# Two attention blocks on one core: a list scheduler that runs in rounds and orders by latest start

## The chip, the cores and the metric

The kernel runs on one core of one Trainium2 chip. A core has a matrix engine (TensorE, PE in the profile, with its weight loads as PEld), a vector engine (DVE), a scalar engine (ACT), a general engine (POOL) and a queue engine (SP) that issues most of the transfers. The metric is the time of one execution on the device in microseconds, as the median of several runs; lower is better.

## The reference

Two conditioned attention blocks follow each other, both over x with 8 batches, 512 positions and 512 features. Each has its own weights. Cut to what matters:

```python
# block 0: linear attention, 8 heads of 64
xn = ln(x)
q = softmax(heads(xn @ Wq + bq), axis=features)
k = softmax(heads(xn @ Wk + bk + mask), axis=positions)
v = heads((xn @ Wv + bv) * mask)
y = q @ (k^T v)
x = x + silu(ln(y) * (1 + scale) + shift) @ W_out + b_out     # scale, shift from silu(emb) @ W_emb
# block 1: full attention, 16 heads of 32
xn = ln(x)
att = softmax(q k^T + mask, axis=keys)
y = att @ v
out = x + silu(ln(y) * (1 + scale) + shift) @ out_w + out_b
```

## The kernel before

**Tiles.** A batch is four chunks of 128 positions by 512 features. Float32 products of projections are made of three passes in the fast float32r format (`project`, line 743): high parts by high, high by low, low by high, 12 matmuls of 512 columns for one output tile.

**Block 0** goes batch by batch: keys and their softmax, values, the 64x64 products of keys and values, queries, outputs.

**Block 1** goes by head groups: G = 4b + g is batch b and its group g of four heads, 32 groups in all. For each group

- `l1_qk` (930) projects keys and queries and writes their high and low parts (hl) to DRAM (dWk, dWq); `l1_stack` (945) loads them back as stacks kst and qst, three buffers each;
- `l1_max` (956) makes scores in the S banks, 16 matmuls, and DVE takes each one's row maximum (nm, a TENSOR_REDUCE). The maxima of a group, split in two parts (mi), are transposed, copied to z, and a small transfer writes them as extra rows into the query stack (qst<-z);
- `l1_att` (982) makes the transposed scores in the ST banks, 16 matmuls, with the maxima subtracted by those extra rows, and ACT takes the exponential into A buffers;
- `l1_av` (1003) multiplies four exponentials with the values, as four matmuls of 32 output rows each that lie side by side in the array (tile a; the trace has two matmul instructions for each, so eight in a group). The exponentials of the later chunks are added onto those of the first (A<-A,A, on POOL or DVE, whichever the planner picks);
- `l1_den` (1032) multiplies those sums with a selector (eg) for the denominators (tile d), again four narrow matmuls.

Beside it run the projections of the next batch and the tail of the one before (transposes, tanh, output product, residual), in the mm banks.

**What sets the order.** Nothing is issued while the program above runs. Every call goes to `Order` (172), which records an operation with its engine, the tiles that it touches and a planned duration from `_takes` (381). A `together` block (186) makes one operation of several matmuls, with a duration given by hand. At the end `place` (262) plays the whole program through: an operation is offered when its dependences are placed and its buffers free; a tag's buffers go out strictly in program order; among the operations that an engine could start, it takes the one with the lowest key, and the key is the place in the program (`o.seq`). A transfer is planned with 560 ns of issue, then a shared rate of 330 bytes per ns and 1700 ns to land. `issue` (361) then writes out every engine's instructions in the order of the planned start; the chip follows this order on each engine and queue. A later user of a tile depends in the plan on that tile's first user (`touch`, 237), transfers included. All instructions have line 370 in the profile, that of the one call that issues them:

```python
engine = getattr(nc, o.takes[o.engine][0])
for method, args, kw in o.calls:
    args = [a.real() if isinstance(a, View) else a for a in args]
    kw = {k: v.real() if isinstance(v, View) else v for k, v in kw.items()}
    getattr(engine, method)(*args, **kw)
```

Buffers: 11 of A, 4 of xc (x and y chunks), 3 of y, 1 of z, 6 of the large stk (raw weights, stacks). Banks: 2 of mm, 2 of S, 2 of ST, 1 of a, 1 of d.

The program starts with block 0's first batch: x and the raw weights (rawL0Wk and so on) are loaded on SP, the small rows of layer norm weights, biases and masks (A<-in_L_cond_ln_b, A<-in_mask_BxSx_fk) too (`load_cols`, 455), and `prep_cols` (468) transposes these and copies them to cols.

Of the kernel before, what the change touches and what calls it, by code (L numbers as in the profile page):

```python
# [4 lines left out]

# [66 lines left out]
class Tile:  # L72
    def __init__(self, pool, tag, shape, dtype, name):
        self.pool, self.tag, self.shape, self.dtype, self.name = pool, tag, tuple(shape), dtype, name
        self.slot, self.ap, self.seen, self.left, self.end = None, None, [], 0, 0.0
        self.view = View(self, (), _index(self.shape), dtype)

    def root(self):
# [13 lines left out]
        return ap  # L92


class View:
# [3 lines left out]
    def _then(self, what, args, kw, at, dtype=None):  # L99
        return View(self.tile, self.chain + ((what, args, kw),), at, dtype or self.dtype)  # L100

    def __getitem__(self, i):
        return self._then("__getitem__", (i,), {}, self.at[i])

    def rearrange(self, pattern, **sizes):
        return self._then("rearrange", (pattern,), sizes, _rearranged(self.at, pattern, sizes))

    def bitcast(self, dtype):
        return self._then("bitcast", (dtype,), {}, self.at, dtype)

    def unsqueeze(self, d):
        return self._then("unsqueeze", (d,), {}, np.expand_dims(self.at, d))

    def broadcast_to(self, shape):
        return self._then("broadcast_to", (shape,), {}, np.broadcast_to(self.at, shape))

    def box(self):
        row = int(np.prod(self.tile.shape[1:]))
        p, c = self.at // row, self.at % row
        return int(p.min()), int(p.max()), int(c.min()), int(c.max())  # L120

    def real(self):
        ap = self.tile.root()
        for what, args, kw in self.chain:
            ap = getattr(ap, what)(*args, **kw)
        return ap


class Pool:
    def __init__(self, order, pool, dram=False, psum=False, each=1, mixed=()):  # L130
        self.order, self.pool, self.dram, self.psum = order, pool, dram, psum
        self.mixed, self.each, self.bufs, self.tiles, self.home = mixed, each, {}, {}, {}

    def tile(self, shape, dtype, name, tag=None, bufs=None):
        tag = name if self.dram else tag or name
# [28 lines left out]
    )  # L164


LINK = {"PE": 55.0, "ACT": 36.0, "DVE": 36.0, "POOL": 90.0, "SP": 60.0}
WEIGHTS = 110.0
DMA_ISSUE, DMA_LAND, DMA_RATE = 560.0, 1700.0, 330.0


class Order:
# [37 lines left out]
    def add(self, name, calls, takes, late, nbytes=0):  # L210
        if not isinstance(takes, dict):
            takes = {name: takes}
        o = Op()
        o.seq, o.calls, o.late, o.bytes = len(self.ops), calls, late, nbytes
        o.takes = {ENGINES[k]: (k, v) for k, v in takes.items()}
        o.deps, o.users, o.tiles, o.fresh = set(), [], [], []
        o.start = o.end = o.engine = None
        o.key = o.seq if self.key is None else self.key
        for t in self.hold:
            self.touch(o, t, None, True)  # L220
        self.hold = []
        for method, args, kw in calls:
            outs, ins = [args[0]], list(args[1:])
            for k, v in kw.items():
                (outs if k == "accum_out" else ins).append(v)
            for v in ins:
                if isinstance(v, View):
                    self.touch(o, v.tile, v.box(), False)
            for v in outs:
                if isinstance(v, View):  # L230
                    box = v.box()
                    if method == "matmul":
                        box = (*box[:2], 0, 511)
                    self.touch(o, v.tile, box, True)
        self.ops.append(o)

    def touch(self, o, t, box, write):
        if t not in o.tiles:
            o.tiles.append(t)
            if t.left:  # L240
                o.deps.add(t.first)
            else:
                o.fresh.append(t)
                t.first = o
            t.left += 1
        if box is None:
# [12 lines left out]
        kept.append((o, box, write))  # L259
        t.seen = kept  # L260

    def place(self):

        now = {e: 0.0 for e in ENGINES.values()}
        ready = {e: [] for e in now}
        later = {e: [] for e in now}
        slots = {}
        dma = 0.0
        for p in self.pools:
            for tag in p.tiles:  # L270
                n = len(p.tiles[tag]) if p.dram else p.bufs[tag]
                slots[p, tag] = [[(0.0, i) for i in range(n)], 0, {}]
        for o in self.ops:
            o.waits = len(o.deps)
            for d in o.deps:
                d.users.append(o)

        def offer(o):

            asked = {}  # L280
            for t in o.fresh:
                room = slots[t.pool, t.tag]
                n = asked.get((t.pool, t.tag), 0)
                if t.place != room[1] + n or len(room[0]) <= n:
                    room[2][room[1] if t.place == room[1] + n else t.place] = o
                    return
                asked[t.pool, t.tag] = n + 1
            at = 0.0
            for t in o.fresh:
                room = slots[t.pool, t.tag]  # L290
                free, t.slot = heapq.heappop(room[0])
                room[1] += 1
# [7 lines left out]
            for e in o.takes:  # L300
                heapq.heappush(later[e], (at, o.seq, o))
            for t in o.fresh:
                room = slots[t.pool, t.tag]
                nxt = room[2].pop(room[1], None)
                if nxt is not None:
                    offer(nxt)

        for o in self.ops:
            if not o.waits:
                offer(o)  # L310
        done = 0
        while done < len(self.ops):
            best = None
            for e in now:
                while later[e] and later[e][0][0] <= now[e]:
                    _, _, o = heapq.heappop(later[e])
# [13 lines left out]
                if best is None or at < best[0]:  # L330
                    best = (at, e, o)
            assert best, "nothing can be placed"
            at, e, o = best
            o.engine, o.start = e, at
            takes = o.takes[e][1]
            if e == "PE" and at > now[e] + 1.0:
                o.start += WEIGHTS
                at = o.start
            now[e] = at + takes
            if o.late is None:  # L340
                dma = max(dma, now[e]) + o.bytes / DMA_RATE
# [4 lines left out]
            for t in o.tiles:  # L346
                t.left -= 1
                t.end = max(t.end, o.end)
                if not t.left:
                    room = slots[t.pool, t.tag]  # L350
                    heapq.heappush(room[0], (t.end + 60.0, t.slot))
                    nxt = room[2].pop(room[1], None)
                    if nxt is not None:
                        offer(nxt)
            for u in o.users:
                u.waits -= 1
                if not u.waits:
# [23 lines left out]
def _takes(engine, method, args, kw):  # L381
# [30 lines left out]
def kernel(ctx: ExitStack, tc: tile.TileContext, x, cond, mask0, mask1, w0, w1, out):  # L412
# [947 lines left out]
```

## Time and profile before

| | before |
|---|---|
| median of 3 runs | 1522.73 us (1520.66 to 1522.84) |
| the profiled execution | 1527.23 us |
| its span, first to last instruction | 1525.2 us |
| mean granted TensorE clock | 0.970 |
| PE busy | 1430.8 us (94%) |
| DVE busy | 1076.0 us (71%) |
| DMA moved | 156.65 MB, mean 103 GB/s |

A row of groups reads: line, engine, operation, output and inputs by name, shapes, count, then busy time, the mean of one in ns, and the idle time ahead of it with what ended it. A row of waits reads: who waited, for whom, microseconds in total, times, the longest. A row of the timeline reads: start, length, instruction, and in brackets the idle time ahead of it.

### The profile page before, as it was taken

Reading aid. Unit: us, or ns where it says so; the run is one execution under the profiler, and the core shown is the slowest. Engines: PE = TensorE matmul, PEld = TensorE weight load, DVE = VectorE, ACT = ScalarE, POOL = GpSimd, SP = SyncE. Lnnn points to the kernel's source line nnn. Section 1 sums busy time; section 2 is a strip of 40 time slices with the busy share of each in tenths; the row PEclk is TensorE's granted clock in tenths of the full one; section 3 lists DMA queues with packets and bytes.
Section 4 is the critical chain, followed back from the end, with each engine's and each line's share of the span. In section 5 each row is a group of like instructions: output and inputs, shape, how many; then the busy total and the mean of one; then the engine's idle time right before and its main releaser. Section 6 shows DMA issues by size and latency. Waiting matters only on the chain.

```text
span 1525.2 us, 20716 instructions
## 1 busy us (share of the span) xinstructions
PE 1430.8 (94%) x7385; PEld 963.0 (63%) x7385; DVE 1076.0 (71%) x1844; ACT 691.3 (45%) x1302; POOL 623.6 (41%) x671
## 2 busy tenths in 40 slices
PE   5899999999999998999899999899999999999997
PEld 2688878888887675545556556455556556656545
DVE  6366655666667677888767678767777867867886
ACT  3223423333335233545555554554545555655562
POOL 3212214124122233455445545445344654554661
PEclk9899999999999998999899999999899999999998
DMA  8014102022121274442263352444435435425311
GB/s 290 13 55 139 52 32 84 1 83 77 63 84 63 86 221 110 143 120 67 86 172 87 108 156 73 134 125 109 122 107 132 126 85 157 127 74 161 86 55 46
DMA packets 76475, 156.65 MB, mean 103 GB/s; under 512 B 8670, under 2 KB 8782, under 8 KB 76372
## 3 DMA queue, kind: packets, MB, share of 16 engines
q1 hardware_dynamic: 73920, 150.99, 33.8%
q10 hardware_dynamic: 2164, 4.24, 0.8%
q8 instruction: 58, 0.95, 0.3%
q14 instruction: 45, 0.37, 0.1%
q0 software_dynamic: 288, 0.10, 0.0%
HBM read 102.67 MB, written 50.40 MB: 100 GB/s over the span
## 4 chain that ended last, share of the span: by engine, by line
PE 77%; DVE 12%; DMA 6%; ACT 2%; issue 1%; POOL 1%; SPq 0%; ACTq 0%; DVEq 0%; POOLq 0%
PE mm L370 46%; PE S L370 11%; PE ST L370 9%; PE a L370 9%; DVE nm L370 4%; DMA qst<-z 3%; DVE A L370 2%; PE d L370 2%; DVE y L370 1%; DVE mi L370 1%; DVE v L370 1%; DMA xc<-in_x 1%; DVE xc L370 1%; ACT A L370 1%; DMA weL<-in_L_cond_W_emb 1%
## 5 line engine op out<-in xcount | busy, mean ns | idle before, releaser
L370 POOL TENSOR_TENSOR A<-A,A 128x512 f32<-128x512 f32 x213 | 303.1, 1439 | 319.4 <-PE a L370 177.6
L370 DVE TENSOR_REDUCE nm<-S 128x1 f32<-128x512 f32 x510 | 339.2, 684 | 101.4 <-PE S L370 99.2
L370 ACT ACTIVATE A<-ST 128x512 f32<-128x512 f32 x448 | 258.9, 603 | 179.0 <-PE ST L370 163.7
L370 PE MATMUL S<-kst,qst 98*128 98x512 f32 x510 | 217.2, 440 | 23.2 <-DVE nm L370 20.3
L370 PE MATMUL ST<-qst,kst 106*128 106x512 f32 x512 | 213.5, 434 | 14.9 <-DMA qst<-z 12.7
L370 PEld LDWEIGHTS S<-kst,qst 98*128 98x128 f32 x510 | 97.5, 194 | 115.1 <-DVE nm L370 76.2
L370 PEld LDWEIGHTS ST<-qst,kst 106*128 106x128 f32 x512 | 96.5, 194 | 86.9 <-ACT A L370 30.5
L370 PE MATMUL a<-A,v 128*32 128x512 f32 x896 | 144.6, 643 | 0.9 <-DVE v L370 0.9
L370 POOL TENSOR_TENSOR y<-y,bo 128x512 f32<-128x512 f32 x60 | 79.6, 1333 | 131.9 <-DMA y<-in_x 90.7
L370 DVE TENSOR_TENSOR A<-A,A 128x512 f32<-128x512 f32 x107 | 104.9, 982 | 39.1 <-PE a L370 31.6
L370 PE MATMUL mm<-xT,Wkh 128*128 128x512 f32 x384 | 118.9, 412 | 6.7 <-DVE cols L370 6.0
L370 PE MATMUL mm<-Wvh,xT 128*128 128x512 f32 x384 | 118.1, 407 | 2.0 <-ACT v L370 1.6
L370 DVE TENSOR_TENSOR y<-y,mm 128x512 f32<-128x512 f32 x60 | 41.1, 685 | 84.4 <-PE mm L370 61.8
L370 PEld LDWEIGHTS mm<-xT,Wkh 128*128 128x128 f32 x384 | 71.9, 194 | 25.1 <-DVE cols L370 6.5
L370 PEld LDWEIGHTS mm<-Wvh,xT 128*128 128x128 f32 x384 | 70.7, 189 | 20.0 <-ACT v L370 2.8
L370 DVE SCALAR_TENSOR_TENSOR v<-bWv,cols,v 128x512 f32<-128x512 f32 x64 | 57.7, 901 | 34.1 <-ACT v L370 33.7
L370 PE MATMUL mm<-Woh,h 128*128 128x512 f32 x224 | 76.0, 437 | 3.8 <-ACT h L370 3.8
L370 ACT ACTIVATE v<-mm,cols 128x512 f32<-128x512 f32 x64 | 44.2, 691 | 71.0 <-PE mm L370 71.0
L370 PE MATMUL mm<-xT,Wqh 128*128 128x512 f32 x256 | 74.5, 398 | 0.0
L370 ACT ACTIVATE hl<-mm,bcol 128x512 fp32r<-128x512 f32 x64 | 43.9, 686 | 62.8 <-PE mm L370 50.8
L370 POOL MEMSET bWk<- 64x4 f32 (+1 forms) x24 | 5.8, 243 | 159.3 <-PE ST L370 158.6
L370 DVE SCALAR_TENSOR_TENSOR hl<-mm,bcol,hl 128x512 fp32r<-128x512 f32 x64 | 47.7, 745 | 27.8 <-ACT hl L370 27.3
(228 smaller groups left out, 2784.2 us busy)
## 6 DMA issues: line engine op xcount, KB each, us to landing
kst<-dWk SPq DMA_DIRECT2D x96, 256.0 KB
qst<-dWq SPq DMA_DIRECT2D x96, 256.0 KB
dWk<-hl SPq DMA_DIRECT2D x32, 512.0 KB
dWq<-hl SPq DMA_DIRECT2D x32, 512.0 KB
xc<-in_x SPq DMA_DIRECT2D x32, 256.0 KB
y<-in_x SPq DMA_DIRECT2D x32, 256.0 KB
x<-y SPq DMA_DIRECT2D x32, 256.0 KB
xc<-x SPq DMA_DIRECT2D x32, 256.0 KB
```

The lines of the kernel that those rows point to most:

```text
L370: getattr(engine, method)(*args, **kw)
```

## The change

`place` now runs up to 12 rounds. Each round plays the program through (`pack`, the old `place` with its keys), then `slack` goes backward over the finished plan and gives every operation as its new key the latest time at which it could start without making the end later, with gaps kept for each engine; the next round orders by these keys. The round with the earliest planned end is kept. The planner also counts, on PE, the cost of going into a group of narrow matmuls and out of it. Some durations change. `l1_den` is no longer an operation of its own: its four matmuls are put ahead of the four of the next head group's first product, in one operation. `Room` replaces the list that hands out buffers; it can hand them out in another order for tags that a pool names as `loose`, and no pool names one. The views' index arrays are cached on the host.

```diff
+ENTER, LEAVE = 95.0, 150.0
+ROUNDS = 12
 LINK = {"PE": 55.0, "ACT": 36.0, "DVE": 36.0, "POOL": 90.0, "SP": 60.0}
...
+class Room:
+    def __init__(self, n, loose):
+        self.free, self.loose, self.head, self.gone, self.queue = [(0.0, i, None) for i in range(n)], loose, 0, set(), {}
+    def lets(self, place, taken):
+        free = len(self.free) - taken
+        if place == self.head + taken:
+            return free > 0
+        return self.loose and free > 1
...
-    def place(self):
+    def place(self, rounds=ROUNDS):
+        best = None
+        for _ in range(rounds):
+            end = self.pack()
+            if best is None or end < best[0]:
+                best = end, [(o.start, o.end, o.engine, [t.slot for t in o.fresh]) for o in self.ops]
+            self.slack(end)
...
+    def slack(self, end):
+        free = {e: [end] for e in ENGINES.values()}
+        for o in sorted(self.ops, key=lambda o: (o.end, o.seq), reverse=True):
+            takes, spent = o.takes[o.engine][1], o.end - o.start
+            t = end - spent
+            for u in o.users:
+                lag = spent + LINK[u.engine]
+                if o.late is not None and o.engine == u.engine:
+                    lag = takes
+                t = min(t, u.key - lag)
+            for x in o.tiles:
+                if x.next is not None:
+                    t = min(t, x.next.first.key - spent - 60.0)
+            o.key = self.latest(free[o.engine], t, takes)
...
-            if e == "PE" and at > now[e] + 1.0:
-                o.start += WEIGHTS
-                at = o.start
+            if e == "PE":
+                many = len(o.calls) > 1
+                if at > now[e] + 1.0:
+                    o.start += WEIGHTS
+                elif many != narrow:
+                    o.start += ENTER if many else LEAVE
+                narrow, at = many, o.start
...
-        return max(62.0, n * (0.447 if args[1].dtype == F32R else 1.668))
+        return max(62.0, n * (0.455 if args[1].dtype == F32R else 1.668))
...
         if n < 64:
-            return 200.0
+            return 400.0 if args[0].tile.tag == "mi" else 200.0
         t = 150.0 + 1.045 * n
         if method == "scalar_tensor_tensor":
             t += 65.0
         if method == "tensor_tensor" and not any(isinstance(a, View) and a.tile.pool.psum for a in ins):
             t += 135.0
+            if args[0].tile.tag == "A":
+                t += 60.0
+        if method == "scalar_tensor_tensor" and not any(isinstance(a, View) and a.tile.pool.psum for a in ins):
+            t += 100.0
         return t
     if engine == "POOL":
         if n < 64:
-            return 1020.0 if ALU.pow in args else 195.0
-        return {"tensor_tensor": 2.66, "tensor_scalar": 1.6}.get(method, 1.03) * n
+            return 900.0 if ALU.pow in args else 350.0
+        return {"tensor_tensor": 2.75, "tensor_scalar": 1.6}.get(method, 1.03) * n
...
     def l1_av(G, m):
         b, g = divmod(G, 4)
-        if m == 0 and G > 0:
-            l1_den(G - 1)
...
-        with order.together(985.0):
+        with order.together(845.0 if m or not G else 1690.0):
+            if m == 0 and G > 0:
+                l1_den(G - 1)
             for j in range(4):
...
     def l1_den(G):
-        with order.together(900.0):
-            for j in range(4):
-                nc.tensor.matmul(
-                    den[32 * j : 32 * j + 32, :], eg[:, g, :], acc[j], start=(g == 0), stop=(g == 3)
-                )
+        for j in range(4):
+            nc.tensor.matmul(
+                den[32 * j : 32 * j + 32, :], eg[:, g, :], acc[j], start=(g == 0), stop=(g == 3)
+            )
...
     l1_av(NG - 1, NC - 1)
-    l1_den(NG - 1)
+    with order.together(845.0):
+        l1_den(NG - 1)
```

More of the change, by code (lines that the diff above doesn't have):

```diff
@@ L2 @@
 import re
+from bisect import bisect_left
 from contextlib import ExitStack, contextmanager
@@ L74, in __init__ @@
         self.pool, self.tag, self.shape, self.dtype, self.name = pool, tag, tuple(shape), dtype, name
-        self.slot, self.ap, self.seen, self.left, self.end = None, None, [], 0, 0.0
+        self.slot, self.ap, self.seen, self.left, self.end, self.next = None, None, [], 0, 0.0, None
         self.view = View(self, (), _index(self.shape), dtype)
@@ L92, in root @@
         return ap
+_SEEN = {}
 class View:
@@ L97, in __init__, with _then @@
         self.tile, self.chain, self.at, self.dtype, self.shape = tile, chain, at, dtype, at.shape
[L99 to L100 removed]
+    def _then(self, what, args, kw, find, dtype=None):
+        chain = self.chain + ((what, args, tuple(kw.items())),)
+        key = self.tile.shape, chain
+        if key not in _SEEN:
+            _SEEN[key] = find()
+        return View(self.tile, chain, _SEEN[key], dtype or self.dtype)
     def __getitem__(self, i):
[L103 removed]
+        return self._then("__getitem__", (i,), {}, lambda: self.at[i])
     def rearrange(self, pattern, **sizes):
[L106 removed]
+        return self._then("rearrange", (pattern,), sizes, lambda: _rearranged(self.at, pattern, sizes))
     def bitcast(self, dtype):
[L109 removed]
+        return self._then("bitcast", (dtype,), {}, lambda: self.at, dtype)
     def unsqueeze(self, d):
[L112 removed]
+        return self._then("unsqueeze", (d,), {}, lambda: np.expand_dims(self.at, d))
     def broadcast_to(self, shape):
[L115 removed]
+        return self._then("broadcast_to", (tuple(shape),), {}, lambda: np.broadcast_to(self.at, shape))
     def box(self):
[L118 to L120 removed]
+        key = self.tile.shape, self.chain, "box"
+        if key not in _SEEN:
+            row = int(np.prod(self.tile.shape[1:]))
+            p, c = self.at // row, self.at % row
+            _SEEN[key] = int(p.min()), int(p.max()), int(c.min()), int(c.max())
+        return _SEEN[key]
     def real(self):
@@ L124, in real, with __init__ @@
         for what, args, kw in self.chain:
-            ap = getattr(ap, what)(*args, **kw)
+            ap = getattr(ap, what)(*args, **dict(kw))
         return ap
 class Pool:
-    def __init__(self, order, pool, dram=False, psum=False, each=1, mixed=()):
+    def __init__(self, order, pool, dram=False, psum=False, each=1, mixed=(), loose=()):
         self.order, self.pool, self.dram, self.psum = order, pool, dram, psum
-        self.mixed, self.each, self.bufs, self.tiles, self.home = mixed, each, {}, {}, {}
+        self.loose, self.mixed, self.each, self.bufs, self.tiles, self.home = loose, mixed, each, {}, {}, {}
     def tile(self, shape, dtype, name, tag=None, bufs=None):
@@ L169, with take, next @@
 DMA_ISSUE, DMA_LAND, DMA_RATE = 560.0, 1700.0, 330.0
+class Room:
[6 more added lines that the diff above has]
+        return self.loose and free > 1
+    def take(self, place):
+        self.gone.add(place)
+        while self.head in self.gone:
+            self.gone.discard(self.head)
+            self.head += 1
+        return heapq.heappop(self.free)
+    def next(self):
+        if self.free and self.head in self.queue:
+            return self.queue.pop(self.head)
+        if self.loose and len(self.free) > 1 and self.queue:
+            return self.queue.pop(min(self.queue))
 class Order:
@@ L234, in add @@
                     self.touch(o, v.tile, box, True)
+        for d in o.deps:
+            d.users.append(o)
         self.ops.append(o)
@@ L243, in touch @@
                 o.fresh.append(t)
-                t.first = o
+                t.first, t.count = o, 0
             t.left += 1
+            t.count += 1
         if box is None:
@@ L260, in touch, with latest, pack @@
         t.seen = kept
-    def place(self):
+    def place(self, rounds=ROUNDS):
[5 more added lines that the diff above has]
+            self.slack(end)
+        for o, (o.start, o.end, o.engine, slots) in zip(self.ops, best[1]):
+            for t, t.slot in zip(o.fresh, slots):
+                pass
+        return best[0]
+    def slack(self, end):
[12 more added lines that the diff above has]
+            o.key = self.latest(free[o.engine], t, takes)
+    @staticmethod
+    def latest(gaps, t, takes):
+        i = min(bisect_left(gaps, t + takes), len(gaps) - 1)
+        i += i % 2
+        while True:
+            hi = min(gaps[i], t + takes)
+            lo = gaps[i - 1] if i else -1e12
+            if hi - takes >= lo:
+                break
+            i -= 2
+        if hi == gaps[i]:
+            gaps[i] = hi - takes
+            if gaps[i] == lo:
+                del gaps[i - 1 : i + 1]
+        else:
+            gaps[i : i + 1] = [hi - takes, hi, gaps[i]]
+        return hi - takes
+    def pack(self):
         now = {e: 0.0 for e in ENGINES.values()}
@@ L267, in place @@
         slots = {}
-        dma = 0.0
+        dma, narrow = 0.0, False
         for p in self.pools:
@@ L271, in place @@
                 n = len(p.tiles[tag]) if p.dram else p.bufs[tag]
-                slots[p, tag] = [[(0.0, i) for i in range(n)], 0, {}]
+                slots[p, tag] = Room(n, tag in p.loose)
         for o in self.ops:
-            o.waits = len(o.deps)
-            for d in o.deps:
-                d.users.append(o)
+            o.waits, o.start = len(o.deps), None
+            for t in o.fresh:
+                t.left, t.end, t.next = t.count, 0.0, None
         def offer(o):
@@ L282, in offer @@
                 room = slots[t.pool, t.tag]
-                n = asked.get((t.pool, t.tag), 0)
-                if t.place != room[1] + n or len(room[0]) <= n:
-                    room[2][room[1] if t.place == room[1] + n else t.place] = o
+                n = asked.get(room, 0)
+                if not room.lets(t.place, n):
+                    room.queue[t.place] = o
                     return
-                asked[t.pool, t.tag] = n + 1
+                asked[room] = n + 1
             at = 0.0
@@ L290, in offer @@
                 room = slots[t.pool, t.tag]
-                free, t.slot = heapq.heappop(room[0])
-                room[1] += 1
+                free, t.slot, before = room.take(t.place)
+                if before is not None:
+                    before.next = t
                 at = max(at, free)
@@ L302, in offer, with again @@
             for t in o.fresh:
[L303 to L306, printed above, removed]
+                again(slots[t.pool, t.tag])
+        def again(room):
+            nxt = room.next()
+            if nxt is not None:
+                offer(nxt)
         for o in self.ops:
@@ L312, in place @@
         while done < len(self.ops):
-            best = None
+            pick = None
             for e in now:
@@ L329, in place @@
                     continue
[L330 to L333, printed above, removed]
+                if pick is None or at < pick[0]:
+                    pick = (at, e, o)
+            assert pick, "nothing can be placed"
+            at, e, o = pick
             o.engine, o.start = e, at
             takes = o.takes[e][1]
-            if e == "PE" and at > now[e] + 1.0:
-                o.start += WEIGHTS
-                at = o.start
+            if e == "PE":
[5 more added lines that the diff above has]
+                narrow, at = many, o.start
             now[e] = at + takes
@@ L350, in place @@
                     room = slots[t.pool, t.tag]
[L351 to L354, printed above, removed]
+                    heapq.heappush(room.free, (t.end + 60.0, t.slot, t))
+                    again(room)
             for u in o.users:
```

## The prediction

> **What bounds the kernel now.** I read the page first: busy shares, the slices, then the chain that ended last.
>
> ```profile
> PE 1430.8 (94%) x7385; PEld 963.0 (63%) x7385; DVE 1076.0 (71%) x1844; ACT 691.3 (45%) x1302; POOL 623.6 (41%) x671
> ...
> PE   5899999999999998999899999899999999999997
> ...
> PEclk9899999999999998999899999999899999999998
> ...
> PE 77%; DVE 12%; DMA 6%; ACT 2%; issue 1%; POOL 1%; SPq 0%; ACTq 0%; DVEq 0%; POOLq 0%
> ```
>
> TensorE is the bound: 94% busy and 77% of the chain; DVE, the next, is at 71%. A plan can only remove TensorE's holes and what the holes cost. PEclk dips at the same slices at which PE does. Next, the busy time by stage:
>
> ```profile
> 0.00:48.00 48.00, 26.13 (x70) 13.50 (x71) 28.20 (x53) 14.06 (x23) 17.75 (x50) 0.86 0.70 239
> 48.00:560.00 512.00, 507.90 (x3015) 406.32 (x3014) 321.08 (x658) 178.95 (x308) 129.24 (x208) 1.00 0.22 74
> 560.00:1440.00 880.00, 825.58 (x3972) 502.28 (x3971) 661.98 (x1032) 455.70 (x883) 437.42 (x380) 0.96 0.42 116
> 1440.00:1526.00 86.00, 71.17 (x334) 40.86 (x332) 64.76 (x104) 42.59 (x89) 39.16 (x34) 0.92 0.19 58
> ```
>
> The columns are the stretch, its length, then busy time of PE, weight load, DVE, ACT, POOL, then granted clock. The start has 21.9 us of PE idle (48 - 26.13), layer 0 has 4.1, the attention stage 54.4, the end 14.8: 95 us in all. Layer 0 is full; there is nothing to win there. Then PE's waits:
>
> ```profile
> PE S L370 <- DVE nm L370: 20.3, 37, 1.8
> PE ST L370 <- DMA qst<-z: 12.7, 13, 5.0
> ...
> PE S L370 <- DVE mi L370: 7.9, 8, 1.7
> ```
>
> In the attention stage PE waits for DVE's row maxima (nm), for what DVE makes of them (mi), and for the small transfer that carries them back into the query stack (z). Then the clock, in two stretches right behind holes of 1.3 us each (849.90 and 1226.10 in the timeline), and the start:
>
> ```profile
> 850.00:856.80 6.80, 6.68 (x18) 3.02 (x19) 5.26 (x9) 2.01 (x4) 3.29 (x3) 0.50 0.55 128
> 1225.40:1232.20 6.80, 6.10 (x18) 3.11 (x18) 2.54 (x6) 2.05 (x4) 5.18 (x7) 0.51 0.09 14
> ...
> 29.37 0.32 SPq L370 DMA_DIRECT2D A<-in_mask_BxSx_fk  x1
> ...
> 34.65 0.31 PE L370 MATMUL mm<-ident,A 48*128 48x48 f32 x1 [5.06 <-DMA A<-in_mask_BxSx_fk]
> ...
> 41.69 0.80 PE L370 MATMUL mm<-xT,Wkh 128*128 128x512 f32 x1 [6.00 <-DVE cols L370]
> ```
>
> A short hole is followed by 3.4 to 6.8 us at half clock. At the start PE stands for 11 us behind one 16 KB load that was issued at 29.37, after the 2.25 MB of rawL0Wo, bo and the next batch's x, and behind the copy of what it brought.
>
> **The change, part by part.** No tensor operation is added, removed or resized; what changes is the order on each engine and queue. `loose` is given to no pool, so Room hands out buffers in program order as before, and the view cache acts on the host alone: both cost 0 on the chip. Sums are against the profiled execution: 1527.2 us, span 1525.2; the median of the runs is 1522.7, so I subtract the savings from 1522.7.
>
> *1. Denominators with the next products.* The timeline of PE around a lone d group, and around one that happens to be followed by an a group:
>
> ```profile
> 835.64 0.39 PE L370 MATMUL S<-kst,qst 98*128 98x512 f32 x1
> 835.96 1.07 PE L370 MATMUL d<-A,eg 128*32 128x512 f32 x8
> 836.95 0.50 PE L370 MATMUL S<-kst,qst 98*128 98x512 f32 x1
> ...
> 899.00 1.07 PE L370 MATMUL d<-A,eg 128*32 128x512 f32 x8
> 899.89 1.04 PE L370 MATMUL a<-A,v 128*32 128x512 f32 x8
> 900.86 0.50 PE L370 MATMUL S<-kst,qst 98*128 98x512 f32 x1
> ```
>
> Wide after wide starts at 0.23 us. Entering d takes 0.32, so 0.09 of entry, and d to the next wide matmul is 0.99: alone 1.08, and an a group alone the same, 2.16 for both. Joined: 0.09 + 1.86 = 1.95. Saved 0.21. Counted in the timeline, 26 of the 32 d groups stand alone: 26 x 0.21 = 5.5 us, on the bound engine. What moves are 8 matmuls per group, on PE alone, no DMA, past 1 to 10 us of other matmuls. The added wait is the product group's wait for the last sums: in the trace each d starts 0.3 to 7 us after the last sum ended and 0.9 to 10 us before its a group, so the inputs are there. What it holds longer are four of the eleven A buffers. Today ACT's exponentials wait 163.7 us for PE's scores and 0.8 for POOL's sums, so buffers do not bind; I take 0. If this cover went, one exponential (603 ns) per lone group would be 26 x 0.6 = 16 us lost, the lower bound; a gain from holding buffers longer is excluded.
>
> *2. The start.* Keys are now latest starts, so the four small column loads (0.27 to 0.33 us of SP issue each, 1.2 in all) should pass rawL0Wo x4, bo and xc x4 on the SP queue (4.8 us of issue), which are pushed back by those 1.2 us; xc is not touched before 36.45 and Wo later still; POOL's queue is not passed, and on ACT's queue only the 1 MB embedding loads could go later. Three of the four also wait in the plan for the first one's landing, so the first has to go early. At stake: the 11.1 us of waiting, and 7.25 us of PE work between 34.2 and 47.9 at half clock, half of which (3.6) would come back: 14.7. Next late are ACT's weight splits and the remaining large loads: DMA is 70% busy here. I take 7, between 0 and 14.
>
> *3. Layer 0.* 4.1 us idle in 512: I take 0, bounds -4 to +3. The cover is the constant supply of projections.
>
> *4. Attention.* Idle 54.4 us. To that comes the clock: twelve half-clock windows lie here, together 65 us long with 60 us of PE work, half of it lost, 30 us (the row's clock of 0.96 over 880 us says 35). Pool: 84 us. [...] The rows show 0.50 and 0.51 right behind such holes, with PE at 6.68 of 6.80 us; I go by the trace.
>
> How much of the pool? The planner's durations ran short of the chip. DVE in the stage: sums A,A 982 ns measured, 820 planned, x107: 17.3 us; A,bWk 1023, x22: 4.5; v 1002 against 750, x32: 8.1; y,z 1028 against 750, x29: 8.1; together 38 us late. New values (880, 850) close 15 of it. PE's narrow groups: 1.08 measured, planned 0.985 (x128) and 0.90 (x32): about 18 us, all closed by 0.845 + 0.095 + 0.150. So some 33 of 56 us of error, 0.6, goes. Waits that DVE ends (nm 20.3, mi 7.9) are half of the 54. 0.6 x 0.5 = 0.3; later keys also let slack be used up and open new waits, so I take a quarter: 21 us[...]. Bounds: half the pool, 42, and -16 from buffers. The z transfers lie on the same SP queue with stack loads of 256 KB; their planned landing is not changed, so of the 12.7 us nothing is counted.
>
> *5. The end.* 14.8 us idle and 5 of half clock. From the last product group (1491.85) it is a serial chain through normalisation, transposes and output that a key cannot shorten; only leftover projections before it can move. I take 2, bounds -3 to +6.
>
> Sum: 5.5 + 7 + 0 + 21 + 2 = 35.5 us; 1522.7 - 35.5 = 1487 us.
>
> **The rivals.** *Only the sure parts* (0.26): the old order was already greedy, taking any ready operation when PE was free, and buffers still go out in program order. Then the holes are the chip's deviations from the plan, which a new order moves but doesn't fill. Den 5.5, start 5, attention 2: 1510. For it: nm holes come singly and short, 1.8 us at most. Against: the wait of 11 us at the start was no deviation; the plan had it, for it issued that load late.
>
> *Slower* (0.13): ordering by latest start uses up the slack that hid DVE's and POOL's overruns. DVE's sums are still planned 100 ns short, and one next to POOL took 1.37 us (847.88). Place: S waiting for nm with two banks. Price: a hole of 1.3 us plus half of a 6.7 us window, 4.6 us each. Parts 1, 2 and 5 give 14.5 us, so more than three extra windows decide it; eight give 37 - 14.5 = 22 slower, 1545. For it: twelve such windows exist now. Against: the refit makes DVE's load in the plan larger, not smaller.
>
> *No effect* (0.04): the best round is the first, which still orders by program order, and the loads stay: den alone against small losses, 1521.
>
> **How the numbers follow.** The forecast case has 0.57. Faster by over 0.2% (3 us, about what a measurement of this kernel can tell from no change): 0.57 + 0.26 = 0.83; within 0.2%: 0.04; slower 0.13. The range: low end with den 5.5, start 14, attention 42, end 5, 66 us: 1456, with 0.07 below it. The high end takes in the sure-parts case and the unchanged one, 1523, with 0.12 above it.
>
> **What would show it.** Right: no d group without an a group behind it; PE's waits on the mask load and on cols before 48 us gone or under 5 us; attention idle from 54 to about 42 and eight or nine half-clock windows instead of twelve; PE's wait on nm nearer 12 than 20. Wrong: the same number of windows with the same nm wait (then the sure parts remain), ACT's exponentials waiting for DVE or POOL sums instead of for PE (buffers), or z transfers landing later because the SP queue stands behind a wait.

## The result, and the profile after

| | before | after |
|---|---|---|
| median of the runs | 1521.7 us (1520.0 to 1522.8) | 1507.45 us (1504.2 to 1511.5) |
| ratio, 95% interval | | 0.9909 (0.9881 to 0.9937) |
| the profiled execution | 1527.2 us, span 1525.2 | 1504.2 us, span 1502.4 |

The change gains 14 us of the 35 that were forecast. Direction and place were right; the size was not. One thing about the two profiles first: before's is slower than all its timed runs, after's is the fastest of its own. Their spans are 22.8 us apart, the medians 14.3. So the profiles show where time went; sizes are taken from ratios of many runs.

The page of the changed kernel, the same rows as before: busy shares, slices, clock, chain.

```profile
PE 1422.8 (95%) x7385; PEld 958.5 (64%) x7385; DVE 1072.2 (71%) x1836; ACT 692.7 (46%) x1302; POOL 635.2 (42%) x679
...
PE   5999999999999998989999999999999999999997
...
PEclk9999999999999999998999999999999999999998
...
PE 76%; DVE 12%; DMA 7%; ACT 3%; issue 2%; POOL 1%; SPq 0%; ACTq 0%; DVEq 0%; POOLq 0%
```

The bound is the same and a little fuller, and the clock row has one digit below 9 ahead of the last slice where it had four, one of these at the start. By stage (length, then PE, weight load, DVE, ACT, POOL, clock):

```profile
0.00:48.00 48.00, 31.19 (x103) 16.94 (x104) 29.11 (x56) 16.54 (x30) 16.68 (x48) 1.00 0.70 240
48.00:560.00 512.00, 510.26 (x3007) 406.22 (x3006) 322.43 (x666) 177.40 (x304) 134.39 (x214) 1.00 0.23 77
560.00:1440.00 880.00, 831.02 (x4045) 506.05 (x4044) 670.64 (x1037) 471.66 (x916) 458.33 (x397) 0.97 0.42 116
```

In the first 48 us PE does 33 matmuls more than before, at full clock; in the 880 us of attention it is idle 49 us, not 54, and does 73 more matmuls. The waits of PE:

```profile
PE S L468 <- DVE nm L468: 13.7, 30, 1.3
PE ST L468 <- DMA qst<-z: 12.2, 14, 1.8
PE S L468 <- DVE xc L468: 10.1, 3, 6.9
PE S L468 <- DVE mi L468: 8.2, 8, 1.9
PE mm L468 <- DMA A<-in_L_cond_ln_b: 6.3, 1, 6.3
```

The wait on the row maxima went from 20.3 to 13.7, those on z and mi did not move. At the start the waits on the mask load (5.06) and on cols (6.00) are gone; the mask load is issued at 16.64 us, not at 29.37. PE now stands once for 6.9 us on xc. Its wait on another small load, in_L_cond_ln_b, was there before and is shorter, 6.3 us; before:

```profile
PE mm L370 <- DMA A<-in_L_cond_ln_b: 8.4, 1, 8.4
```

The operations of the score tiles give the stage borders (the last two figures ahead of the semicolon are the first and the last start), before and then after:

```profile
L370 PE MATMUL ST<-qst,kst x512: 389/401/797, 592.7 to 1489.7; 106*128 106x512 f32 x171
L370 PE MATMUL S<-kst,qst x510: 388/400/797, 558.7 to 1490.5; 98*128 98x512 f32 x170
```

```profile
L468 PE MATMUL ST<-qst,kst x512: 388/400/796, 586.0 to 1465.4; 106*128 106x512 f32 x171
L468 PE MATMUL S<-kst,qst x510: 388/401/797, 553.9 to 1473.2; 98*128 98x512 f32 x170
```

Up to the first score S the profiled execution gains 4.8 us, from there to the first ST 1.9, from the first to the last ST 17.6 (897.0 to 879.4), and from there to the end it loses 1.5 (35.5 to 37.0 of span): 22.8.

### The profile page after: what moved, and what is told of

The parts are those of the page before. It is cut to its first block, busy times and chain, and to the rows that moved or that the text cites. A ratio compares the mean times of both kernels' runs of the same rounds, so it can differ in the third digit from the quotient of the medians.

```text
span 1502.4 us, 20747 instructions
## 1 busy us (share of the span) xinstructions
PE 1422.8 (95%) x7385; PEld 958.5 (64%) x7385; DVE 1072.2 (71%) x1836; ACT 692.7 (46%) x1302; POOL 635.2 (42%) x679
## 4 chain that ended last, share of the span: by engine, by line
PE 76%; DVE 12%; DMA 7%; ACT 3%; issue 2%; POOL 1%; SPq 0%; ACTq 0%; DVEq 0%; POOLq 0%
PE mm L468 45%; PE S L468 11%; PE ST L468 9%; PE a L468 9%; DMA qst<-z 4%; DVE nm L468 4%; PE d L468 2%; DVE A L468 1%; DVE y L468 1%; DVE mi L468 1%; ACT z L468 1%; DVE v L468 1%; ACT A L468 1%; DVE h L468 1%; ACT y L468 1%
## 5 line engine op out<-in xcount | busy, mean ns | idle before, releaser
L468 POOL TENSOR_TENSOR A<-A,A 128x512 f32<-128x512 f32 x223 | 321.8, 1459 | 324.0 <-PE a L468 200.7
L468 PE MATMUL ST<-qst,kst 106*128 106x512 f32 x512 | 210.7, 433 | 13.8 <-DMA qst<-z 12.2
L468 DVE TENSOR_TENSOR A<-A,A 128x512 f32<-128x512 f32 x97 | 94.7, 979 | 52.3 <-PE a L468 40.5
L468 PE MATMUL mm<-xT,Wkl 128*128 128x512 f32 x192 | 62.3, 404 | 0.0
```

## The experiments

All ratios are against the kernel before, measured beside each kernel on the same chip; 0.001 is 1.5 us. In brackets are 95% intervals. Each profile is one execution of its kernel.

**1. The parts, one at a time.** The joining alone, on the kernel before:

```diff
 # the kernel before
-        if m == 0 and G > 0:
-            l1_den(G - 1)
-        with order.together(985.0):
+        with order.together(985.0 if m or not G else 1885.0):
+            if m == 0 and G > 0:
+                l1_den(G - 1)
```

> The kernel before with only the denominators joined to the next products (planned 985 + 900 = 1885 ns); keys and durations as before. If joining saves 0.21 us on the bound engine in 26 of 32 groups, as predicted: 5.5 us less than before, about 1516. If joining is paid back, because the sums are held longer and the first product of a group waits for them: 1522 or more, with PE idle in the attention stage above 54 us.

Measured: 1.0062 (1.0037 to 1.0086), 9 us slower. Its attention stage and waits:

```profile
560.00:1440.00 880.00, 818.12 (x3900) 499.49 (x3898) 650.05 (x1013) 443.99 (x861) 428.77 (x369) 0.95 0.41 113
```

```profile
PE S L370 <- DVE nm L370: 22.2, 46, 1.8
PE ST L370 <- DMA qst<-z: 16.9, 17, 5.2
PE S L370 <- DVE mi L370: 12.2, 12, 2.2
```

PE's idle time rose from 54 to 62 us, 46 holes on nm instead of 37, and half-clock windows cover 85 us of the stage instead of 65. All 31 pairs stand together, and each pair does save its 0.2 us (a median of 1.85 us from d to the next wide matmul, as in the pair of the prediction); the holes take more.

One round, everything else as changed:

```diff
 # the changed kernel
-ROUNDS = 12
+ROUNDS = 1
```

> The changed kernel with one round in place of twelve: new durations and joined denominators, but program order as the key. If the new keys carry the gain: 1516 to 1520, with the wait of 11 us at the start back. If the durations and the joining carry it (my rival of the sure parts, where a new order fills nothing): 1507, as with twelve rounds.

Measured: 1.0095 (1.0069 to 1.0121). With program order as the key the new durations and the joining together make the kernel 14 us slower. Both expectations missed this, and the 11 us at the start did not come back: the mask load is issued at 19.39 here. Against 0.9909, the rounds are worth 28 us, and they carry all of the gain. That part of my "sure parts" rival falls: a greedy order leaves much for a better one.

The denominators apart again, and then the old durations, each in the changed kernel:

```diff
 # the changed kernel: denominators apart
-        with order.together(845.0 if m or not G else 1690.0):
-            if m == 0 and G > 0:
-                l1_den(G - 1)
+        if m == 0 and G > 0:
+            with order.together(845.0):
+                l1_den(G - 1)
+        with order.together(845.0):
```

> The changed kernel with the denominators as operations of their own again (845 ns each), all else as changed. If joining is worth what it saves on PE: 5 us slower than the changed kernel, about 1512, with some 25 groups standing alone. If it is paid back in held buffers: 1507 or less.

Measured: 0.9903 (0.9881 to 0.9925). The same as joined.

```diff
 # the changed kernel: _takes as before, and
-ENTER, LEAVE = 95.0, 150.0
+ENTER, LEAVE = 0.0, 0.0
-        with order.together(845.0 if m or not G else 1690.0):
+        with order.together(985.0 if m or not G else 1885.0):
```

> The changed kernel with twelve rounds and joined denominators, but all durations as before (no cost of entering and leaving narrow groups, 985 and 1885 ns for them). If the keys alone carry the gain: 1507 to 1511. If a plan by latest start only holds on the chip when its durations are right: 1518 or more, with PE waiting longer for nm than the 13.7 us of the changed kernel.

Measured: 0.9865 (0.984 to 0.989), 1502.8 us: the rounds do better with the old durations than with the new. Neither expectation said this.

The rounds alone (old durations, denominators apart):

> The kernel before with the twelve rounds alone: old durations, denominators apart. Theory (the keys gain about 29 us, joining costs up to 8 and the new durations about 6): 0.980 to 0.984 of before, some 1495. Rival (with the rounds in place joining costs nothing, as the pair with new durations said): the same as with joined denominators and old durations, 0.9865 of before.

Measured: 0.9866 (0.9848 to 0.9884), as with joined denominators. With the rounds the joining costs nothing and brings nothing that these intervals of 3 us could tell, twice measured. The rounds by themselves are 20 us; joining adds 0 to that and the new durations take away some 6. In the profile of the rounds alone the time from the first to the last ST falls by 23.5 us (897.0 to 873.5), PE is idle for 44.5 us of the attention stage instead of 54.4, and its half-clock windows cover 34 us instead of 65.

**2. Which of the durations loses.** The new durations on PE only, then on DVE and POOL only:

```diff
 # the changed kernel, _takes as before except
-        return max(62.0, n * (0.447 if args[1].dtype == F32R else 1.668))
+        return max(62.0, n * (0.455 if args[1].dtype == F32R else 1.668))
```

> Rounds, joined denominators, new durations on PE only (845 and 1690 ns with entry and exit costs, 0.455 ns per column), old ones on DVE, POOL. If the loss of the new durations comes from PE's: 0.991 of before, as the changed kernel. If it comes from those of DVE and POOL: 0.9865, as with old durations.

> The other half: rounds, joined denominators, old durations on PE (985 and 1885 ns, no entry or exit cost), new ones on DVE and POOL. If the loss comes from these: 0.991 of before, with more sums on POOL. If from PE's: 0.9865.

Measured: PE's 0.9848 (0.9835 to 0.986), DVE's and POOL's 0.9969 (0.9953 to 0.9985). The loss comes from the second. So I added these to the PE durations in three parts:

```diff
 # on the kernel with PE's new durations, one at a time
+        if method == "scalar_tensor_tensor" and not any(... psum ...):    # stt
+            t += 100.0
...
+            if args[0].tile.tag == "A":                                  # sums
+                t += 60.0
-        return {"tensor_tensor": 2.66, ...
+        return {"tensor_tensor": 2.75, ...
...
-            return 200.0                                                # small
+            return 400.0 if args[0].tile.tag == "mi" else 200.0
-            return 1020.0 if ALU.pow in args else 195.0
+            return 900.0 if ALU.pow in args else 350.0
```

> The kernel with rounds, joined denominators and new durations on PE only, and to these the one new duration of DVE's scalar_tensor_tensor without a PSUM operand (+100 ns). All of DVE's and POOL's new durations together cost some 12 us beside old PE durations. If this one (it stands in both layers' values and hidden parts) carries it: 0.991 to 0.994 of before, with layer 0's narrow products split into more runs. If none of them matters alone, or the loss is the luck of one order: 0.985, as with PE's alone.

> The same base with the new durations of the sums alone (DVE +60 ns for A, POOL 2.75 for 2.66 ns per element). If these carry the loss: 0.991 to 0.994, with a changed share of sums on POOL, and the loss in the attention stage. If not: 0.985.

> The same base with the new durations of the small operations alone (mi 400 for 200 ns, where the trace has 177; POOL's small ones 350 for 195, its power 900 for 1020). mi is the one value set away from the measurement. If it carries the loss: 0.991 to 0.994, with mi's waits no shorter. If padding mi helps the row that PE waits for: below 0.985 and PE's wait on mi under 4 us.

Measured: the value for scalar_tensor_tensor (stt from here on) 0.9945 (0.9923 to 0.9967), sums 0.9822 (0.9803 to 0.9841), small 0.9811 (0.9789 to 0.9832), against 0.9848 without. One value loses 15 us; the others gain 4 and 6. The first 48 us, without and with the small values:

```profile
0.00:48.00 48.00, 27.54 (x90) 15.63 (x91) 27.08 (x54) 15.27 (x27) 18.78 (x50) 0.96 0.70 240
```

```profile
0.00:48.00 48.00, 33.82 (x120) 19.18 (x121) 29.92 (x59) 18.17 (x33) 19.31 (x53) 1.00 0.71 240
```

PE does 6.3 us more work at the start. mi is not used before 586 us, and PE's wait on it is 3.6 us against 4.2; so the gain is more likely that of POOL's small values than of the 400 ns for mi. The two were not tried apart. Then the changed kernel without stt's value:

```diff
 # the changed kernel
-        if method == "scalar_tensor_tensor" and not any(... psum ...):
-            t += 100.0
```

> The changed kernel without the +100 ns of scalar_tensor_tensor, all else as changed. If this one duration is what the new durations lose: 0.981 to 0.983 of before, as with the sums or the small operations added to PE's. If the parts don't add up (luck of each order): anywhere from 0.983 to 0.992.

Measured: 0.9803 (0.9779 to 0.9826), 1494.0 us. The one line takes back 0.0106, 16 us, about as much as the change gained.

**3. Why that value loses.** The groups of DVE in the kernel with PE's new durations, cut to layer 0 (108 to 550 us) and to attention (590 to 1466); the columns after the bar are busy time and mean of one:

```profile
L468 DVE SCALAR_TENSOR_TENSOR v<-bWv,cols,v 128x512 f32<-128x512 f32 x28 | 22.7, 810 | 23.5 <-ACT v L468 23.0
L468 DVE SCALAR_TENSOR_TENSOR y<-y,z 128x512 f32<-128x512 f32 x30 | 20.7, 691 | 8.1 <-ACT z L468 8.1
```

```profile
L468 DVE SCALAR_TENSOR_TENSOR v<-bWv,cols,v 128x512 f32<-128x512 f32 x28 | 28.5, 1017 | 1.7 <-ACT v L468 1.6
L468 DVE SCALAR_TENSOR_TENSOR y<-y,z 128x512 f32<-128x512 f32 x28 | 24.9, 888 | 2.4 <-ACT z L468 2.4
```

The same instruction takes 691 to 810 ns in layer 0 and 888 to 1017 in attention. 850 for both is near a mean over the kernel and wrong in layer 0: by 159 ns for y where the old 750 was wrong by 59, by 40 for v where it was wrong by 60. What makes the duration differ is in the last section. With the 100 ns in layer 1 alone:

```diff
 # the changed kernel
-            t += 100.0
+            t += 0.0 if args[0].tile.name.startswith(("vL0", "sl")) else 100.0
```

> The changed kernel with the +100 ns in layer 1 alone, where 1002 and 1028 ns were measured, and 750 in layer 0, where 690 and 810 were. If the value is bad because it is wrong for layer 0: layer 0 4 to 5 us shorter, with 27 runs of narrow products instead of 34, and 0.984 to 0.987 of before. If it is bad in the attention stage too: 0.989 to 0.991.

Measured: 0.9866 (0.9841 to 0.989). Without the value in layer 0 the kernel is 0.0043 or 6.6 us faster, by the intervals some 1 to 12; in the profiles the stretch from the second batch's last key product to the first S is 3.7 us shorter (452.2 to 448.5). The rest, the larger part, is lost elsewhere: between the profiles of the changed kernel and of the one without the value, the time from the first to the last ST falls by 9.5 us (879.4 to 869.9). In attention 850 is nearer to the mean than 750, and why it loses there stays open. How the value works in layer 0 is seen in PE's timeline of one batch of stt, the products of keys and values:

```profile
179.58 0.33 PE L468 MATMUL a<-v,A 128*64 128x64 f32 x2
181.77 0.56 PE L468 MATMUL a<-v,A 128*64 128x64 f32 x10
182.92 0.33 PE L468 MATMUL a<-v,A 128*64 128x64 f32 x2
192.71 1.61 PE L468 MATMUL a<-v,A 128*64 128x64 f32 x46
196.10 0.33 PE L468 MATMUL a<-v,A 128*64 128x64 f32 x2
197.38 0.33 PE L468 MATMUL a<-v,A 128*64 128x64 f32 x2
```

These are narrow matmuls too, 64 instructions per batch, but single operations for the planner; ENTER and LEAVE are charged to `together` blocks alone. In this kernel the plan scatters them into six runs, and each run pays a change of width: the two at 182.92 start 0.32 us after the wide matmul ahead of them, where wide after wide starts at 0.23, and the next wide one starts 0.26 us after the first of the two. In the kernel with the products kept together, further down, 64 of them in one run take 2.01 us up to the next wide one, 0.03 each. Counted from the second batch's last key product to the first S, there are 23 runs of narrow products before (two of them belong to layer 1's set-up), 27 with PE's new durations, 34 in the changed kernel, 35 in stt, and 27 with the value in layer 1 alone. Kept together:

```diff
 # on the kernel with PE's new durations and the 100 ns
 def l0_att(b):
+        with order.together(2300.0):
             for i in range(4):
                 for c in range(NC):
                     for u in range(2):
```

> PE's new durations and the +100 ns in both layers (0.9945), with each batch's 32 products of 64 columns in layer 0 made one operation of 2300 ns. If the loss in layer 0 is the split of these products, for which the plan charges nothing: layer 0 5 us shorter and 0.990 to 0.991. If the split only goes with a later supply: no change, or longer, since all 32 now wait for the last value.

Measured: 0.9925 (0.9901 to 0.995) against 0.9945, within each other's intervals. The timeline of the same stretch has one run, and from the second batch's last key product to the first S, layer 0 is 6.5 us shorter, first stt, then with the products together:

```profile
104.40:558.50 454.10, 451.39 (x2644) 360.83 (x2643) 287.96 (x583) 161.46 (x274) 127.58 (x198) 1.00 0.24 78
```

```profile
103.90:551.50 447.60, 444.66 (x2643) 358.69 (x2642) 289.28 (x583) 160.42 (x274) 127.25 (x198) 1.00 0.25 79
```

With PE's new durations and without the value the same stretch takes 448.9 us. So the split is what the value costs in layer 0, some 5 us: the same matmuls, 6.7 us less of PE busy time. In that profile the attention stage gave the gain back (882.4 us from first to last ST, then 890.9). But stt's profile is the fastest of its nine runs, 8.5 us under their median, so these two attention stages can't be compared.

Is it luck of each order instead? One duration changed by 1 ns:

```diff
 # on the kernel with PE's new durations
-        t = 178.0 + 0.82 * n
+        t = 179.0 + 0.82 * n
```

> PE's new durations alone (0.9848), and ACT's base 179 for 178 ns, which says nothing about the chip. If a new order has luck of its own: away from 0.9848 by 0.003 or more. If orders of nearly equal durations take nearly equal time: 0.983 to 0.987.

Measured: 0.9858 (0.9835 to 0.9882) against 0.9848. The new order moved the time by 1.5 us, well under the 15 of stt. It is a single draw. The whole set says more. Of the kernels with twelve rounds and mm banks in program order, five have the 100 ns in both layers: 0.9903, 0.9909, 0.9925, 0.9945, 0.9969. Seven don't have it: 0.9803, 0.9811, 0.9822, 0.9848, 0.9858, 0.9865, 0.9866. They differ in other durations and in joining, so they are twelve orders, and the two groups don't overlap; the kernel with the value in layer 1 alone, 0.9866, stands at the edge. The luck of one order can't explain that; a few us between two kernels it can.

**4. A version that beats both.** Loose mm banks, which the change provides and doesn't use, on the rounds alone; and then with PE's new durations:

```diff
 # rounds, old durations, denominators apart
-    ps = order.pool(..., psum=True)
+    ps = order.pool(..., psum=True, loose=('mm',))
```

> A version that may beat both: rounds, old durations, denominators apart, and the two mm banks handed out loosely, so that a projection that is ready can pass one that waits. If program order of the mm banks holds the plan back: 8 to 14 us under the kernel with the rounds alone, with PE's waits at the batch borders shorter. If the holes are the chip's deviations from the plan: the same as with the rounds alone, or slower because the added crossings wait for each other.

> The best so far (rounds, denominators apart, loose mm banks) with the new PE durations in place of the old. If right PE durations help as they did with joined denominators (0.9848 against 0.9865): 0.974 to 0.976 of before, 1486 or less. If they do nothing: 0.9765.

Measured: 0.9765 (0.9749 to 0.9782), and with PE's durations 0.9831 (0.9812 to 0.9851). The first is 15 us faster than the rounds alone, and PE's durations take 10 of them back. Without loose banks they had made 2.6 us, which is within the intervals: the parts don't add.

The same loose banks with the sums and small durations (first), and on the changed kernel without stt's 100 ns (second):

> Rounds, loose mm banks, denominators apart, old PE durations (0.9765) with the new durations of the sums and of the small operations. If these gain here as they did on the base without loose banks (0.0026 and 0.0037): 0.970 to 0.974. If the plan with loose banks is at its end: 0.9765.

> The changed kernel without the +100 ns (0.9803), with loose mm banks. If the banks' order holds this plan back as it did the one with old durations (0.9866 to 0.9765): 0.970 to 0.973. If what PE's new durations took from the loose banks (0.9831) is general: 0.979 to 0.984.

Measured: 0.9742 (0.9725 to 0.9758), 1485.8 us, and 0.9754 (0.9739 to 0.9769). The first has the lowest time of all, though its interval overlaps the second's, and neither expectation for the second came out: loose banks brought it 0.0049, half of the 0.0101 that they brought to the rounds alone. In the first one's attention stage

```profile
560.00:1440.00 880.00, 836.75 (x4141) 505.82 (x4140) 691.36 (x1058) 483.56 (x945) 482.80 (x414) 0.99 0.43 117
```

PE is idle 43 us, and does 169 more matmuls in the same 880 us than the kernel before.

## Why the prediction was wrong

*Step 4, the refit, is the step that failed.* I worked out that the new durations close 0.6 of the plan's error and put a quarter of the pool, 21 us, on that. Beside the rounds, the new durations together cost 6.6 us (0.9866 without, 0.9909 with them). I took the measured durations from the attention stage alone and gave layer 0 a zero, "the constant supply of projections" being its cover. But the 100 ns for scalar_tensor_tensor hold in both layers, and in layer 0 they scatter the narrow products, 35 runs in place of 27 and some 5 us beside PE's new durations. That one value costs 16 us of the kernel; the part lost in attention has no shown cause. Without it the kernel stands at 0.9803, 30 us below before. A value nearer to its mean isn't worth what the error sum says. The sum itself had a small slip, 880 and 850 close 13.8 us of DVE's error and not 15, and a larger flaw: the means in it mix two cases. In the kernel before, y<-y,z took 682 ns in the 11 of 27 cases with no POOL instruction beside it and 1423 in the 11 beside one of POOL's sums.

*Step 1, joining, +5.5.* The saving per pair is there; in the end it measures 9 us slower alone and 0 beside the rounds. The bound "16 us lost, through held buffers" had the sign, hardly the cause: ACT's exponentials wait 5.7 us on POOL's sums in that kernel, 0.8 before. Nor do the holes stand behind the joined groups: of the 46 waits on nm only one, of 0.3 us, begins within 5 us of a joined group's d. Why joining loses in program order stays open.

*What I underrated is the change's own core.* The rounds alone bring 20 us, and 28 to 30 in pairs that also have the joining. I had put them down only through the start (7) and a share of the pool. The forecast's sum missed by 21 us: 16 by stt, 5.5 by joining. That the rest fits is partly luck, since refit and rounds were misattributed against each other.

*Step 2, the start, +7.* The number came out, the mechanism only in part. The named waits left, the clock went from 0.86 to 1.00, and PE's busy time in the first 48 us rose by 5.1 us (26.13 to 31.19). With the rounds alone the mask load is issued early too, at 16.81, and both waits are gone; but one on another load takes their place, and PE's busy time there rises by 1.4 us only:

```profile
PE mm L468 <- DMA A<-in_L_cond_ln_b: 16.9, 1, 16.9
```

```profile
0.00:48.00 48.00, 27.55 (x89) 15.48 (x90) 27.13 (x54) 15.06 (x26) 18.79 (x50) 0.96 0.70 240
```

The new small durations shorten that wait to 6 us (17.0 without them, beside PE's new durations). By the end of the second batch's last key product the rounds alone are 3.5 us ahead of before and the changed kernel 6.9, single profiles all. So about half of the 7 came by the loads, the rest with a part of the change that step 2 did not count, which is luck.

*Step 3, layer 0, 0.* Between the start's gain and the first S some 2 us were lost (450.0 to 452.2 us from the second batch's last key product), inside the bounds of -4 to +3, by the mechanism above.

*Step 5, the end, +2.* It lost 1.5 in the profiles.

*The clock.* I counted nine half-clock windows in attention, 44 us, where before has twelve, 65: as forecast ("eight or nine"). They are 85 us in the slower kernel with joined denominators alone, 27 without stt's 100 ns, and 17 in the fastest. The mean granted clocks of all runs fit: 0.966 to 0.977 before, 0.966 to 0.972 with joining alone, 0.979 to 0.984 for the changed kernel, 0.989 to 0.992 for the fastest. In these four PE is idle in attention for 54, 62, 49 and 43 us, so less idle time went with a higher clock, and it was right to count the lost half clock into the pool. Not in proportion: without stt's 100 ns the idle time is 49 us as well, with 27 us of half clock where the changed kernel has 44. And that a short hole is followed by half clock says too much: 15 of the 37 holes on nm lie neither in a half-clock stretch nor in the 3.4 us ahead of one, one of 1.5 us (659.6) among them. PE's idle time in attention fell to 49 us, not to the 42 that were forecast.

*The rivals.* "Only the sure parts" came out closest in size, 1510, by the wrong route: the joining of 5.5 and the end of 2 were not there. "Slower" is real for this kernel in program order: joining alone costs 9 us, joining with the new durations 14. Its price of 4.6 us per extra window was too high: joining alone has four windows more and costs 9 us, some 2.3 each.

## What to carry to other kernels

A planner's durations are not a fit to be made ever closer to one mean: they steer an order. Test each value alone on the chip, and look at every stage that it governs, above all where nothing seems to be at stake. Before fitting a mean, look at what it is a mean of. Costs that the planner charges to some forms of an operation and not to others (here the change of width, for blocks but not for single matmuls) are where it will push work to. Measure the parts of a change one at a time, in both surroundings: here the same joining was 9 us or nothing.

## What the runs showed of the hardware

The twelve half-clock stretches in attention of the kernel before are 3.4 us long (six), 6.8 (five) or 10.2 (one). In the 3.4 us ahead of eleven of them PE never stood still for more than 1.8 us at a time. The 3.4 us ahead of such a stretch, and the stretch, before and then after (PE busy is the first figure after the length):

```profile
846.60:850.01 3.41, 1.95 (x8) 0.91 (x6) 3.41 (x6) 3.41 (x10) 2.60 (x2) 1.00 0.93 278
850.01:856.84 6.83, 6.71 (x18) 3.05 (x19) 5.25 (x9) 2.00 (x4) 3.27 (x3) 0.50 0.54 127
```

```profile
963.30:966.70 3.40, 1.40 (x7) 0.52 (x6) 3.21 (x5) 3.40 (x10) 2.77 (x4) 1.00 0.89 269
966.70:973.50 6.80, 6.01 (x17) 2.93 (x18) 3.97 (x7) 1.84 (x4) 1.14 (x1) 0.50 0.45 110
```

PE was busy 57% and 41% of the time ahead. Ahead of the twelve of the kernel before, PE's idle share over 3.4 us was between 21 and 58% in these eleven cases and 86% in the other. The idle share alone doesn't decide: here PE was idle for 38%, and full clock (1.00) followed.

```profile
635.04:638.45 3.41, 2.10 (x14) 1.04 (x16) 3.34 (x6) 1.17 (x3) 2.49 (x2) 1.00 0.52 148
638.45:641.87 3.42, 3.42 (x23) 1.34 (x16) 2.27 (x5) 0.97 (x2) 0.00 (x0) 1.00 0.77 175
```

What tells the two cases apart is not shown, nor was it tried whether the same holes cost less when spread out.

DVE's stt of v and y and its sums, with all tensor operands in SBUF, have no one duration in these traces: beside POOL's sums most of them end after these. In the kernel with PE's new durations, y<-y,z takes 0.66 us with no POOL instruction beside it, and 1.78 when it starts just after one of POOL's sums. It then ends 0.55 us after that sum (1099.19 and 1098.64):

```profile
958.77 0.66 DVE L468 SCALAR_TENSOR_TENSOR y<-y,z 128x512 f32<-128x512 f32 x1
```

```profile
1097.36 1.28 POOL L468 TENSOR_TENSOR A<-A,A 128x512 f32<-128x512 f32 x1 [2.95 <-ACT A L468]
1097.41 1.78 DVE L468 SCALAR_TENSOR_TENSOR y<-y,z 128x512 f32<-128x512 f32 x1
```

Counted over 590 to 1466 us of that trace: 21 of the 56 stt of v and y start while a two-input POOL instruction (TENSOR_TENSOR) runs, and 20 of them end 0.55 us after it, whenever they began; so do 72 of 76 of DVE's own sums. The other way round, all 32 such POOL instructions that start during one of these stt end 1.13 to 1.16 us after it. In layer 0 none of the 30 y<-y,z has a POOL instruction beside it, and their mean is 691 ns. The row maxima (nm) and hl, which read PSUM, show no such wait: 224 of nm and 14 of hl start beside such a POOL instruction and take 627 to 694 and 736 to 752 ns, as the others do.
